# Building an attention row once and broadcasting it by DMA, instead of transposing a broadcast on TensorE

## The chip, the cores and the metric

The kernel runs on one core of a Trainium2 chip. The core has five engines that matter here: TensorE (PE, with its weight loads shown as PEld), VectorE (DVE), ScalarE (ACT), GpSimd (POOL) and SyncE (SP, which only issues DMA transfers here). The metric is the device time of one execution in microseconds; before the change it is 3412.09 us, the median of three runs (3411.46 to 3415.26). The profile is of another execution and spans 3416.2 us.

## The reference, cut to what matters

Four graph-attention layers run over `x` of shape (32, 512, 256): 32 batches of 512 tokens with 256 features, all float32. Each layer normalizes its input and adds its result to it. In shape, all four do this:

```python
h = maximum(layernorm(x), 0)
Wh = h @ W                               # 512 tokens x 256 features
s_i, s_j = Wh @ a1, Wh @ a2              # one number for each token
e = leaky_relu(s_i[:, None] + s_j[None, :])
e = where(mask, e, -inf)                 # mask: adjacency, the same for all batches
out = elu_or_relu(softmax(e, axis=-1) @ Wh)
x = x + out
```

Layer 2 does it with four heads of 64 features. Layer 3 has a small network around it and two attentions: one on 512 features without a mask, one on 256 with it.

The softmax weight before normalization, exp(leaky_relu(s_i + s_j)), is a maximum of two products of exponentials. A factor that depends on i alone cancels in the softmax, and a factor of j can be put on the rows of `Wh`. What is left for each pair is `max(R_i, T_j) * mask`: a row `R` over the tokens i, and a column `T` over the tokens j.

## The kernel before

Tokens lie on the 128 partitions in NT = 4 tiles, so `R` comes out of the value projection as a column: one number for each partition, in each of the four tiles. The weights `w[j, i]` need it along the free dimension and the same on all partitions. The kernel gets that from TensorE: it takes the column of one token tile, broadcasts it to 128 x 128 with a step of zero and transposes that against the identity. Four such transposes, one for each token tile, fill a PSUM bank with `R` (128 x 512). VectorE reads it there, four times, and writes the four tiles of `w`:

```python
def weights(r_col, t_col, masked=True):
    r = bank()                                             # one PSUM bank, of 8
    for t in range(NT):
        nc.tensor.transpose(r[:, t * P:(t + 1) * P], r_col(t).to_broadcast([P, P]), ident)
    wt = work.tile([P, NT, N], FP, tag="w", name="w", bufs=5)
    for j in range(NT):
        if masked:
            nc.vector.scalar_tensor_tensor(
                wt[:, j, :], r, t_col(j), maskT[:, j, :], op0=OP.max, op1=OP.mult)
        else:
            nc.vector.tensor_scalar(wt[:, j, :], r, t_col(j), None, op0=OP.max)
    return wt

def aggregate(p, wt, t, rhs):                              # the attention times the values
    for j in range(NT):
        nc.tensor.matmul(p, wt[:, j, t * P:(t + 1) * P], rhs(j), start=(j == 0), stop=(j == NT - 1))

def plain(hT, w):                                          # layers 0, 1 and the second of layer 3
    v = yield from values(hT, w)                           # projection; columns F.. hold the exponentials
    wt = weights(lambda t: v[:, t, F + 2:F + 3], lambda j: v[:, j, F + 1:F + 2])
    yield
    return v, wt
```

Layer 2 calls `weights` once for each of its four heads. The first attention of layer 3 calls it without a mask, and then goes on like this:

```python
    ys = []
    for t in range(NT):
        y, q = pair(), pair()
        # ... aggregate, reciprocal, two activations ...
        elu2_plus1(y, q)                                   # VectorE, ScalarE, and last GpSimd
        ys.append(y)
        yield
    for f in range(KH):                                    # 4 feature blocks
        p = bank()
        for t in range(NT):
            nc.tensor.transpose(p[:, t * P:(t + 1) * P],
                ys[t].rearrange("p a f -> p (a f)")[:, f * P:(f + 1) * P], ident)
        nc.vector.scalar_tensor_tensor(oT[:, f, :], p, -1.0, oT[:, f, :], op0=OP.add, op1=OP.add)
        # ...
```

Each batch is a Python generator that goes through the four layers and yields between steps. Four such streams run in turn, each started 20 rounds after the one before it, so that at the start one stream is alone, then two, then three:

```python
live = []
for i in range(NS):                                        # NS = 4
    live.append(stream(i))                                 # batches i, i + 4, i + 8, ...
    if i + 1 < NS:
        for _ in range(LEAD):                              # LEAD = 20
            for g in live:
                next(g)
# ... then all four in turn to the end
```

A scheduler then decides, when the kernel is built, in which order the instructions stand on each engine; each engine runs its own in that order. All DMA transfers are issued from SyncE: the inputs and weights at the start, then one load of `x` and one store of the output for each batch.

Of the kernel before, what the change touches and what calls it, by code (L numbers as in the profile page):

```python
# [19 lines left out]
FP = mybir.dt.float32  # L20
# [3 lines left out]
OP = mybir.AluOpType  # L24
# [3 lines left out]
P = 128  # L28
# [5 lines left out]
def fast(ctx, tc, flag, x, adj, w0, a0, w1, a1, w2, a2, mlp1_w, mlp1_b, mlp2_w, mlp2_b,  # L34
# [14 lines left out]
    psum = ctx.enter_context(tc.tile_pool(name="psum", bufs=1, space=bass.MemoryType.PSUM))  # L49

# [31 lines left out]
    def project(dst, block, kt, a_cols):  # L82

        ft, n = a_cols.shape[1], a_cols.shape[2]
        for k in range(kt):
# [3 lines left out]
            wT = work.tile([P, N], FP, tag="y", name="wT", bufs=8)  # L89
# [54 lines left out]
    raw2 = work.tile([P, KF, F], FP, tag="y2", name="raw2", bufs=4)  # L144
# [94 lines left out]
    def weights(r_col, t_col, masked=True):  # L239

        r = bank()
        for t in range(NT):
            nc.tensor.transpose(r[:, t * P:(t + 1) * P], r_col(t).to_broadcast([P, P]), ident)  # L243
        wt = work.tile([P, NT, N], FP, tag="w", name="w", bufs=5)
        for j in range(NT):
            if masked:
                nc.vector.scalar_tensor_tensor(  # L247
                    wt[:, j, :], r, t_col(j), maskT[:, j, :], op0=OP.max, op1=OP.mult
                )
            else:  # L250
                nc.vector.tensor_scalar(wt[:, j, :], r, t_col(j), None, op0=OP.max)
        return wt

    def pair():
        return work.tile([P, 2, F], FP, tag="y", name="y", bufs=8)
# [10 lines left out]
    def plain(hT, w):  # L266
        v = yield from values(hT, w)
        wt = weights(lambda t: v[:, t, F + 2:F + 3], lambda j: v[:, j, F + 1:F + 2])
# [20 lines left out]
    def layer0(xt):  # L289
        v, wt = yield from plain((yield from norm_t(xt)), W0)  # L290
        for t0 in range(0, NT, 2):
            r, q = pair(), pair()
# [18 lines left out]
    def layer2(xt):  # L311
# [15 lines left out]
        note(v.rearrange("p t h c -> p (t h) c")[:, :, D:])  # L327
        ys = [pair(), pair()]
        for h in range(NH):
            wt = weights(lambda t: v[:, t, h, D + 2:D + 3], lambda j: v[:, j, h, D + 1:D + 2])  # L330
# [12 lines left out]
        for i in range(2):  # L343
            y, q = ys[i], pair()
# [5 lines left out]
    def layer3(xt):  # L350
# [18 lines left out]
        wt = weights(lambda t: v[:, t, F + 2:F + 3], lambda j: v[:, j, F + 1:F + 2], masked=False)  # L369
        yield  # L370
        ys = []
        for t in range(NT):
            y, q = pair(), pair()
# [8 lines left out]
            ys.append(y)  # L382
            yield
        for f in range(KH):
            p = bank()
            for t in range(NT):
                nc.tensor.transpose(  # L387
                    p[:, t * P:(t + 1) * P], ys[t].rearrange("p a f -> p (a f)")[:, f * P:(f + 1) * P], ident
                )
            nc.vector.scalar_tensor_tensor(oT[:, f, :], p, -1.0, oT[:, f, :], op0=OP.add, op1=OP.add)  # L390
            if f % 2:
                yield
        rT = yield from linear_t(oT, WM2, b2, "rT")
        v, wt = yield from plain(rT, WHA)
        for t0 in range(0, NT, 2):
            y, q = pair(), pair()
# [489 lines left out]
```

## Time and profile before

| what | value |
|---|---|
| time, median of three | 3412.09 us |
| TensorE busy in the profile | 3314.6 us, 97% |
| VectorE, ScalarE, GpSimd busy | 50%, 40%, 17% |
| transposes that build R (line 243) | 1024 |
| VectorE operations that build w (lines 247 and 251) | 896 + 128 |
| DMA traffic | 40.67 MB, mean 12 GB/s |

In the lists that follow, a line such as `L243 PE MATMUL b<-ident,v` is a group of instructions: the source line, the engine, the operation, and output<-inputs by the program's names, `b` being a PSUM bank. After `x` comes the count, then the busy time in us and the mean duration of one in ns, then the idle time of that engine just before them and what ended it. The durations of neighbouring matmuls overlap, so a group's busy time can exceed what it takes in sequence. A float32 matmul is two instructions (two passes), and a transpose is one; so `L259`, the aggregation, counts 9216 for 4608 matmuls in the program. "PEld" is the load of the stationary operand, which overlaps the matmuls.

### The profile page before, as it was taken

The page shows a single profiled execution, that of the slowest core. Times are in us where ns is not written, and L with a number is a line of the kernel's source. Part 1 is how long each engine was busy: PE and PEld are TensorE (multiplying, and loading weights), DVE is VectorE, ACT ScalarE, POOL GpSimd, SP SyncE. Part 2 cuts the span into 40 slices and gives each one's busy share as a digit, 9 for nine tenths or more (in the row PEclk, how much of TensorE's full clock was granted, in tenths as well). Part 3 has the DMA queues.
Part 4 walks back from the last instruction along what each step waited for, and adds up shares of the span by engine and source line. Part 5 has one row for each costly group of instructions (what it writes and reads, how often), then busy time and mean ns, then how long its engine had stood idle before and what let it go on. Part 6 is the DMA issues. An engine that isn't in the chain of part 4 may idle for free.

```text
span 3416.2 us, 44221 instructions
## 1 busy us (share of the span) xinstructions
PE 3314.6 (97%) x17265; PEld 2750.0 (80%) x17265; DVE 1700.9 (50%) x4422; ACT 1380.6 (40%) x3281; POOL 571.7 (17%) x583
## 2 busy tenths in 40 slices
PE   6899999999999999999999999999999999999997
PEld 5688888788887887878878888788888788887875
DVE  3554563554644655446544455454653545635542
ACT  2234434444334434344334443444434444344433
POOL 0111111211112111121111121112201111112111
PEclk8899999999999999999999999999999999999999
DMA  2000000000000000000000000000000000000000
GB/s 80 1 1 13 13 1 13 13 13 13 1 13 13 13 13 1 13 19 7 13 13 1 25 7 7 13 1 25 13 1 13 11 16 13 1 13 7 7 7 14
DMA packets 41606, 40.67 MB, mean 12 GB/s; under 512 B 5296, under 2 KB 40624, under 8 KB 41392
## 3 DMA queue, kind: packets, MB, share of 16 engines
q1 hardware_dynamic: 41392, 37.77, 3.6%
q8 instruction: 140, 2.29, 0.3%
q14 instruction: 74, 0.61, 0.1%
HBM read 20.99 MB, written 16.78 MB: 11 GB/s over the span
## 4 chain that ended last, share of the span: by engine, by line
PE 87%; DVE 6%; ACT 3%; POOL 3%; issue 1%; DMA 0%; SPq 0%; POOLq 0%; ACTq 0%; DVEq 0%
PE b L259 43%; PE b L357 13%; PE b L234 11%; PE b L216 8%; PE b L317 3%; PE b L198 3%; PE b L243 3%; PE b L387 1%; DVE xn L190 1%; POOL y L287 1%; DVE st L182 1%; DVE x L281 1%; POOL rs L186 1%; PE b L405 1%; DVE y L280 1%
## 5 line engine op out<-in xcount | busy, mean ns | idle before, releaser
L259 PE MATMUL b<-v,w 128*128 128x257 f32 (+2 forms) x9216 | 1657.9, 337 | 19.2 <-DVE w L247 16.9
L259 PEld LDWEIGHTS b<-v,w 128*128 128x128 f32 x9216 | 1457.2, 194 | 218.5 <-issue 44.0
L247 DVE SCALAR_TENSOR_TENSOR w<-b,v,maskT 128x512 f32<-128x512 f32 x896 | 609.2, 744 | 37.3 <-PE b L243 37.3
L287 POOL TENSOR_TENSOR y<-y 128x512 f32<-128x512 f32 x192 | 243.4, 1268 | 1799.2 <-ACT y L286 1566.7
L263 DVE RECIPROCAL rden<-b 128x1 f32<-128x1 f32 (+1 forms) x640 | 101.9, 166 | 756.2 <-PE b L259 755.4
L357 PE MATMUL b<-WFC,oT 128*128 128x259 f32 (+1 forms) x2048 | 466.4, 380 | 0.0
L357 PEld LDWEIGHTS b<-WFC,oT 128*128 128x128 f32 x2048 | 381.9, 189 | 62.5 <-issue 8.1
L190 DVE TENSOR_SCALAR xn<-x,mv,rs 128x256 f32<-128x256 f32 x512 | 190.8, 432 | 153.1 <-POOL rs L186 153.1
L216 PE MATMUL b<-W,hT 128*128 128x259 f32 x1024 | 263.4, 402 | 2.1 <-ACT hT L199 2.0
L182 DVE BATCH_NORM_STATS2 st<-x 128x6 f32<-128x256 f32 x512 | 194.4, 406 | 98.3 <-POOL x L308 67.1
L234 PE MATMUL b<-hT,WM 128*128 128x512 f32 x512 | 240.8, 593 | 0.0
L234 PE MATMUL b<-oT,WM 128*128 128x512 f32 x512 | 232.2, 596 | 0.5 <-DVE oT L390 0.5
L216 PEld LDWEIGHTS b<-W,hT 128*128 128x128 f32 x1024 | 195.4, 200 | 34.2 <-ACT hT L199 7.3
L295 ACT ACTIVATE y<-b,rden 128x256 f32<-128x256 f32 x128 | 60.8, 475 | 395.6 <-DVE rden L263 395.6
L379 ACT ACTIVATE y<-b,rden 128x256 f32<-128x256 f32 x256 | 123.2, 481 | 222.7 <-DVE rden L263 173.1
L199 ACT ACTIVATE hT<-b 128x512 f32<-128x512 f32 x256 | 142.3, 595 | 143.7 <-PE b L198 142.5
L221 ACT ACTIVATE v<-b,v 128x256 f32<-128x256 f32 x384 | 182.5, 475 | 12.5
L234 PEld LDWEIGHTS b<-oT,WM 128*128 128x128 f32 x512 | 95.8, 191 | 95.4 <-issue 87.5
L285 DVE TENSOR_SCALAR y<-y 128x512 f32<-128x512 f32 x192 | 82.4, 429 | 178.5 <-ACT y L379 142.4
L364 ACT ACTIVATE v<-b,v 128x256 f32<-128x256 f32 x256 | 121.5, 475 | 117.8 <-PE b L357 113.6
L198 PE MATMUL b<-ident,xn 128*128 128x128 f32 x1024 | 145.0, 283 | 19.1 <-DVE xn L190 19.1
L286 ACT ACTIVATE y<-y,minus 128x512 f32<-128x512 f32 x192 | 138.8, 723 | 57.3 <-DVE y L285 41.4
(99 smaller groups left out, 2892.8 us busy)
## 6 DMA issues: line engine op xcount, KB each, us to landing
x<-in_x_dram SPq DMA_DIRECT2D x32, 512.0 KB, 3.8
out_dram<-x SPq DMA_DIRECT2D x32, 512.0 KB, 2.9
adj<-in_adj_dram SPq DMA_DIRECT2D x1, 1024.0 KB, 8.1
WM<-in_L_gnn_mlp_w_dram SPq DMA_DIRECT2D x2, 512.0 KB, 5.4
WFC<-in_L_gnn_W_fc_dram SPq DMA_DIRECT2D x2, 512.0 KB, 5.7
W<-in_L_gnn_W_dram SPq DMA_DIRECT2D x2, 256.0 KB, 7.8
raw<-in_L_gnn_W_dram SPq DMA_DIRECT2D x1, 256.0 KB, 5.6
WHA<-in_L_gnn_W_hand_dram SPq DMA_DIRECT2D x1, 256.0 KB, 6.2
```

Source lines behind the costliest of these rows:

```text
L182: nc.vector.bn_stats(st[:, t, :], xt[:, t, :])
L190: nc.vector.tensor_scalar(xn[:, t, :], xt[:, t, :], mv[:, t, 0:1], rs[:, t:t + 1], op0=OP.subtract, op1=OP.mult)
L198: nc.tensor.transpose(p[:, t * P:(t + 1) * P], xn[:, t, k * P:(k + 1) * P], ident)
L199: nc.scalar.activation(hT[:, k, :], p, AF.Relu)
L216: nc.tensor.matmul(ps[:, :F + 3], hT[:, k, t * P:(t + 1) * P], w[:, k, :], start=(k == 0), stop=(k == KF - 1))
L221: nc.scalar.activation(v[:, t, :F], ps[:, :F], AF.Copy, scale=pj)
L234: nc.tensor.matmul(p, w[:, k, f * P:(f + 1) * P], inT[:, k, :], start=(k == 0), stop=(k == kt - 1))
L247: nc.vector.scalar_tensor_tensor(wt[:, j, :], r, t_col(j), maskT[:, j, :], op0=OP.max, op1=OP.mult)
L259: nc.tensor.matmul(p, wt[:, j, t * P:(t + 1) * P], rhs(j), start=(j == 0), stop=(j == NT - 1))
L286: nc.scalar.activation(q, q, AF.Exp, bias=minus1)
L287: nc.gpsimd.tensor_tensor(r, r, q, op=OP.add)
L357: nc.tensor.matmul(ps[c][:, :n], oT[:, k, t * P:(t + 1) * P], WFC[:, k, c * (F + 3):c * (F + 3) + n], start=(k == 0), stop=(k == KH - 1),)
```

## The change

`R` is transposed once for all token tiles, and the spreading over the partitions is left to a DMA. A new helper `spread` takes the four columns of `R` (16 in layer 2: four tiles by four heads) as one 128 x n operand, transposes it into n rows of 128, has ScalarE copy them to SBUF, and stores them in a DRAM buffer. `weights` then reads that buffer back with a DMA whose source is broadcast over the 128 partitions, so that `r` lies in SBUF (256 KB over all partitions). It is meant to take the repeated transposes from TensorE and the bank for `R` from PSUM. There is a yield between `spread` and `weights`, so that other streams may run meanwhile.

To make room in SBUF, the tag `y` goes from 8 buffers to 6, `q` gets a tag of its own with 3, and a weight buffer used at the start moves to another tag. In layer 3 the transposes of `y` are done after each token tile, and no longer for all four at the end. The numbers of matmuls there are the same.

```diff
+    dram = ctx.enter_context(tc.tile_pool(name="dram", bufs=1, space=bass.MemoryType.DRAM))
...
-            wT = work.tile([P, N], FP, tag="y", name="wT", bufs=8)
+            wT = work.tile([P, N], FP, tag="y", name="wT", bufs=6)
...
-    raw2 = work.tile([P, KF, F], FP, tag="y2", name="raw2", bufs=4)
+    raw2 = work.tile([P, KF, F], FP, tag="hT", name="raw2", bufs=3)
...
-    def weights(r_col, t_col, masked=True):
-
-        r = bank()
-        for t in range(NT):
-            nc.tensor.transpose(r[:, t * P:(t + 1) * P], r_col(t).to_broadcast([P, P]), ident)
+    def spread(cols):
+
+        n = cols.shape[1]
+        p = bank()
+        nc.tensor.transpose(p[:n, :P], cols, ident)
+        s = work.tile([P, P], FP, tag="row", name="row", bufs=3)
+        nc.scalar.copy(s[:n, :], p[:n, :P])
+        rows = dram.tile([n, P], FP, tag=f"row{n}", name=f"row{n}", bufs=2 * NS)
+        nc.sync.dma_start(rows, s[:n, :])
+        return rows
+
+    def weights(row, t_col, masked=True):
+
+        r = work.tile([P, N], FP, tag="r", name="r", bufs=6)
+        nc.sync.dma_start(r.rearrange("q (t p) -> q t p", p=P), row.partition_broadcast(P))
...
-    def pair():
-        return work.tile([P, 2, F], FP, tag="y", name="y", bufs=8)
+    def pair(tag="y"):
+        return work.tile([P, 2, F], FP, tag=tag, name=tag, bufs=6 if tag == "y" else 3)
...
     def plain(hT, w):
         v = yield from values(hT, w)
-        wt = weights(lambda t: v[:, t, F + 2:F + 3], lambda j: v[:, j, F + 1:F + 2])
+        r = spread(v[:, :, F + 2])
+        yield
+        wt = weights(r, lambda j: v[:, j, F + 1:F + 2])
         yield
... (layer 2)
+        rows = spread(v[:, :, :, D + 2].rearrange("p t h -> p (t h)")).rearrange("(t h) p -> h t p", h=NH)
+        yield
         for h in range(NH):
-            wt = weights(lambda t: v[:, t, h, D + 2:D + 3], lambda j: v[:, j, h, D + 1:D + 2])
+            wt = weights(rows[h], lambda j: v[:, j, h, D + 1:D + 2])
... (layer 3, first attention)
-        wt = weights(lambda t: v[:, t, F + 2:F + 3], lambda j: v[:, j, F + 1:F + 2], masked=False)
-        yield
-        ys = []
-        for t in range(NT):
-            y, q = pair(), pair()
+        r = spread(v[:, :, F + 2])
+        yield
+        wt = weights(r, lambda j: v[:, j, F + 1:F + 2], masked=False)
+        yield
+        for t in range(NT):
+            y, q = pair(), pair("q")
...
-            ys.append(y)
-            yield
-        for f in range(KH):
+            yield
             p = bank()
-            for t in range(NT):
+            for f in range(KH):
                 nc.tensor.transpose(
-                    p[:, t * P:(t + 1) * P], ys[t].rearrange("p a f -> p (a f)")[:, f * P:(f + 1) * P], ident
+                    p[:, f * P:(f + 1) * P], y.rearrange("p a f -> p (a f)")[:, f * P:(f + 1) * P], ident
                 )
-            nc.vector.scalar_tensor_tensor(oT[:, f, :], p, -1.0, oT[:, f, :], op0=OP.add, op1=OP.add)
-            if f % 2:
-                yield
+            o = oT[:, :, t * P:(t + 1) * P]
+            nc.vector.scalar_tensor_tensor(
+                o, p.rearrange("p (f c) -> p f c", c=P), -1.0, o, op0=OP.add, op1=OP.add
+            )
+            yield
```

With the added yields a batch has 62 steps, where it had 55; `LEAD` stays 20.

More of the change, by code (lines that the diff above doesn't have):

```diff
@@ L291, in layer0 @@
         for t0 in range(0, NT, 2):
-            r, q = pair(), pair()
+            r, q = pair(), pair("q")
             for i in range(2):
@@ L343, in layer2 @@
         for i in range(2):
-            y, q = ys[i], pair()
+            y, q = ys[i], pair("q")
             nc.scalar.activation(q, y, AF.Exp)
@@ L395, in layer3 @@
         for t0 in range(0, NT, 2):
-            y, q = pair(), pair()
+            y, q = pair(), pair("q")
             for i in range(2):
```

## The prediction

> **What bounds the kernel now.** I read the busy shares first, then the chain of waits, then the groups by line, then a stretch of the timeline, and last the waits and the DMA landings.
>
> ```profile
> span 3416.2 us, 44221 instructions
> ...
> PE 3314.6 (97%) x17265; PEld 2750.0 (80%) x17265; DVE 1700.9 (50%) x4422; ACT 1380.6 (40%) x3281; POOL 571.7 (17%) x583
> ...
> PE 87%; DVE 6%; ACT 3%; POOL 3%; issue 1%; DMA 0%; SPq 0%; POOLq 0%; ACTq 0%; DVEq 0%
> ...
> L243 PE MATMUL b<-ident,v 128*128 128x128 f32 x1024 | 145.7, 273 | 0.0
> ```
>
> ```profile
> 0.00:100.00 100.00, 62.31 (x260) 50.47 (x260) 38.48 (x107) 23.39 (x55) 10.48 (x17) 0.78 0.25 69
> 100.00:3300.00 3200.00, 3155.78 (x16546) 2625.93 (x16546) 1625.56 (x4228) 1313.13 (x3130) 542.30 (x550) 0.98 0.03 10
> 3300.00:3416.00 116.00, 96.55 (x463) 73.57 (x461) 36.91 (x89) 44.07 (x96) 18.96 (x16) 0.95 0.03 10
> ```
>
> TensorE sets the end: 97% busy, 87% of the chain. The second fence cuts the span in three (the columns are the stretch, its length, then PE, PEld, DVE, ACT and POOL busy): PE is idle 38 us in the first 100 us, 44 us in the 3200 us of the middle, and 19 us at the end. So every TensorE microsecond taken out of the middle is worth about one, and every new TensorE wait costs one. The other engines have room.
>
> The group of L243 is what the change attacks: the 1024 transposes that build the row R. Its busy sum, 145.7 us, is too high a price, since neighbouring matmuls overlap. The timeline gives the pace:
>
> ```profile
> 1697.30 0.60 PE L243 MATMUL b<-ident,v 128*128 128x128 f32 x4
> 1697.73 7.15 PE L259 MATMUL b<-v,w 128*128 128x257 f32 x48
> ...
> 1709.06 0.60 PE L243 MATMUL b<-ident,v 128*128 128x128 f32 x4
> 1709.50 1.92 PE L216 MATMUL b<-W,hT 128*128 128x259 f32 x8
> ```
>
> (start, length, what.) Four transposes start at 1697.30 and the next matmul at 1697.73; again 1709.06 and 1709.50. That is 0.435 us for four, 0.109 us each.
>
> ```profile
> DVE w L247 <- PE b L243: 37.3, 27, 2.8
> ```
>
> ```profile
> SPq L64 <- DMA out_dram<-x: 73.3, 27, 4.2
> ```
>
> ```profile
> x<-in_x_dram SPq DMA_DIRECT2D x32, 512.0 KB, 3.8
> out_dram<-x SPq DMA_DIRECT2D x32, 512.0 KB, 2.9
> ```
>
> ```profile
> L247 DVE SCALAR_TENSOR_TENSOR w<-b,v,maskT x896: 723/744/754, 56.5 to 3396.6; 128x512 f32<-128x512 f32 x180
> ...
> L281 DVE SCALAR_TENSOR_TENSOR x<-y,x x128: 661/684/1751, 62.9 to 3327.1; 128x512 f32<-128x512 f32 x128
> ...
> L251 DVE TENSOR_SCALAR w<-b,v x128: 741/746/753, 182.0 to 3364.3; 128x512 f32<-128x512 f32 x128
> ...
> L285 DVE TENSOR_SCALAR y<-y x192: 408/427/1228, 189.7 to 3404.4; 128x512 f32<-128x512 f32 x192
> ```
>
> The waits (total us, times, longest): building w waited for R only 27 times, so today R is at hand almost at once. A store that a later load depends on already costs the SyncE queue 2.7 us a time (73.3 / 27). The last column of the DMA lines is the median from issue to landing. The triples of the last fence are shortest, median and longest in ns.
>
> [...]
>
> [...] L251, from PSUM, 746 ns; L285, from SBUF at the same size, 427.
>
> [...] L281 (two SBUF inputs) has 1751 ns as its longest, median 684; L247 (one input in PSUM) never passes 754. After the change L247's successor has both inputs in SBUF.
>
> **The change, part by part.**
>
> *Removed from TensorE.* Per batch there are eight builds of w (one each in layers 0 and 1, four heads in layer 2, two in layer 3), each with four transposes: 32 batches x 8 x 4 = 1024. In their place are five one-shot transposes per batch (layer 2's four heads share one): 160. Net 864 x 0.109 = 94 us off TensorE, 2.8%.
>
> *Added elsewhere.* 160 ScalarE copies of 128 columns, about 0.27 us each by L90's COPY of 256 columns (373 ns): 43 us on an engine that is 40% busy. 160 stores of 2 or 8 KB and 256 broadcast reads of 256 KB, 416 issues at 0.37 us (the duration of a DMA issue in the trace) on a SyncE queue that is nearly idle: 154 us of 3400. The unmasked w of layer 3 reads SBUF and should fall from 746 to about 430 ns, 128 x 0.32 = 41 us off VectorE, not on the path.
>
> *The new lag.* From the transposes to the first use of w there were about 1.1 us (PE latency 0.16, one VectorE op 0.74, signals). Now: PE 0.16; waiting for ScalarE and its copy 0.5; store 1.9 (the output store's 2.9[...]); broadcast read 2.6 (the 512 KB load's shortest is 2.9, by its tile's answer, and this has half the bytes), or 3.4 for layer 2[...]; VectorE 0.74 and its queue 0.2; signals 0.2. Estimates: 6.3 us for ordinary layers, 7.1 for layer 2, 6.0 for the unmasked one (its first VectorE op is shorter).
>
> *What TensorE has to do meanwhile.* Nobody waits if other streams fill the lag. In the built program's own order on TensorE I added up the work between each new transpose and the first aggregation with its w, at the trace's pace (0.434 us for a 257-column float32 matmul, two passes; 0.22 for 65 columns; 0.86 for 512; 0.109 a transpose). The middle repeats every four batches. Its four layer-2 gaps hold 4.6, 6.2, 7.1 and 10.5 us; the four unmasked ones 7.1, 7.2, 8.9 and 9.3; the twelve ordinary ones 6.9 to 14.4. Against the lags only 4.6 and 6.2 fall short, by 2.5 and 0.9 us; with the next three w, which come 0.74 us apart, the cycle loses about 5 us. At the start one stream runs alone, then two, and at the end again: the gaps there are 0 to 4 us and each spread is exposed. The same sum, end to end: first 400 us 37 us of waits, middle 32, last 400 us 36, together 104. The order of the kernel before, with its lag of 1.1, gives 14, 0 and 14, so 76 us are new.
>
> *Layer 3's tail.* The back transposes of y now follow each token tile instead of coming in one block at the end. TensorE waited 23.8 us for GpSimd's y there; I take half of it, 10 us, as saved. The number of matmuls is the same.
>
> *The PSUM bank* that R occupied through four VectorE ops (3 us, 256 times) is free. Steady PE idle is only 44 us, so I give this nothing.
>
> *GpSimd collisions.* L281's mean is 845 ns against a median of 684: 0.16 us a time. On the 896 masked ops I take 0.1 us, 90 us of VectorE time, of which little is on the path; with the VectorE queue standing still behind a late R: +10 us together.
>
> Sum: 3412 - 94 + 76 - 10 + 10 = 3394; I predict **3395 us**, 0.5% faster.
>
> **The rivals.**
>
> *The lag is hidden (about 3330).* If store and read take 1.5 us less together than I think, the same sum over the order gives 60 us of waits instead of 104, and the end and start shrink too. For it: the gaps of the middle are mostly 7 us and more. Against it: no group of transfers in the trace has a median landing under 2.5 us (the 0.2 KB loads of the layer-2 vector a), and two must run one after the other.
>
> *A new wait takes the place of the work (3440 and more).* With a lag 1 us longer the sum is 145 us, 2 us longer 191: about 45 us per microsecond. For it: SyncE serves its queue in order, and one queue now carries rows of four streams, so a read may stand behind another row's store, or behind an output store that waits for GpSimd; and R's late arrival also stops VectorE's queue. Then 3435 to 3480.
>
> *VectorE becomes the bound.* 1701 + 90 - 41 = 1750 us, 51%: no. [...]
>
> **Range and chances.** The gain of 94 us is sure to within 10. The new waits are the doubt: a lag between 1 us shorter (69 us) and 1.5 longer (about 167) puts the time between 3359 and 3457; with 20 us for collisions and the layer-3 tail below, 3340 to 3460 holds it 8 times in 10. Over 2% faster means under 3344, which needs the lag hidden and the tail smoothed: 0.19. Slower than 3480 needs a lag over 2 us longer than mine: 0.13. Within 2%: 0.68.
>
> **What would show it.** The L244 group should have 160 transposes at about 0.11 us apart, and PE busy should fall by about 90 us. Store landings near 2 us and reads of 2.6 to 3.4 confirm the lag. PE's idle time by releaser should name VectorE's w in front of the aggregation, mostly in layer 2 (65-column form) and in the first and last 400 us; the middle's idle should stay near 70 us or less. The unmasked w should take about 430 ns and the masked ones keep 744 as median with a tail over 1 us. The prediction is wrong if landings are above 4 us, if PE's idle appears in the middle for other reasons (xn, y, a full PSUM), or if TensorE's pace itself changes.

## The result, and the profile after

| kernel | median, us | ratio to before, 95% interval |
|---|---|---|
| before, four runs | 3413.68 | |
| changed, four runs | 3689.33 | 1.0798 (1.0774 to 1.0822) |

The change costs 276 us, 8%. The page of the changed kernel (span and counts, the engines, TensorE's busy share and its granted clock in 40 slices, the chain's shares):

```profile
span 3688.0 us, 43451 instructions
...
PE 3409.4 (92%) x16401; PEld 2794.7 (76%) x16401; DVE 1698.4 (46%) x4422; ACT 1407.1 (38%) x3441; POOL 599.7 (16%) x583
...
PE   5889999989999899999999899998999999998885
...
PEclk7789999999999899999999999998999999998887
...
PE 72%; DVE 10%; DMA 6%; POOL 5%; ACT 4%; issue 2%; SPq 0%; POOLq 0%; ACTq 0%; DVEq 0%
```

TensorE has 864 instructions fewer, as meant, and is nevertheless busy 95 us longer (3409.4 against 3314.6). Its idle time went from 101.6 to 278.6 us (the span less busy). Against the 94 us by which its work should have shrunk, the rest of the work took 189 us more. So the 272 us between the two spans are -94 of work, +177 of idle time and +189 of pace. The clock row shows the pace: it falls under full speed at both ends and now and then in the middle. The span and mean granted clock of the kernel before and of this one:

```profile
core 0: 3416.2 us, clock 0.977
core 0: 3688.0 us, clock 0.927
```

The span times what the clock lacks to 1 is the work at full pace that was lost: 3416.2 x 0.023 = 79 us before, 3688.0 x 0.073 = 269 us here, 190 more. That is the 189 of pace, so next to nothing is left for anything but the clock to slow TensorE. By stretch (stretch, its length, busy time and instructions of each engine, clock, DMA share, GB/s):

```profile
0.00:100.00 100.00, 59.43 (x223) 47.44 (x224) 31.36 (x79) 20.88 (x49) 6.67 (x12) 0.74 0.25 74
100.00:3300.00 3200.00, 3039.93 (x14924) 2501.32 (x14923) 1547.56 (x4052) 1269.33 (x3118) 538.92 (x523) 0.95 0.10 29
3300.00:3688.00 388.00, 310.05 (x1258) 245.90 (x1256) 119.46 (x292) 116.86 (x274) 54.12 (x48) 0.83 0.06 20
```

The middle is idle for 160 us where it was idle for 44, at a clock of 0.95 where it had 0.98. The waits (total us, times, longest):

```profile
DVE w L258 <- DMA r<-row: 218.5, 64, 10.0
...
PE b L401 <- POOL y L300: 131.3, 62, 4.8
...
PE b L270 <- DVE w L258: 76.7, 46, 6.5
```

and the wait for y in the kernel before:

```profile
PE b L387 <- POOL y L287: 23.8, 24, 2.5
```

VectorE waits 218 us for R, and TensorE 77 us for w: the lag of the new route. But the largest wait of TensorE is another one: 131 us for GpSimd's y in front of layer 3's transposes (L401), where it waited 23.8 us before. Of the 177 us of new idle time 108 are for y (131.3 - 23.8) and 63 for w (82.6, both kinds of w together, against 19.3). The aggregation by its forms, and w on VectorE (shortest, median, longest in ns):

```profile
L270 PE MATMUL b<-v,w 128*128 128x257 f32 x4096 | 1012.1, 401 | 45.9 <-DVE w L258 34.5 <-DVE w L262 5.9 <-DVE rden L274 5.5
...
L270 PE MATMUL b<-v,w 128*128 128x65 f32 x4096 | 595.9, 311 | 43.1 <-DVE w L258 42.1
```

The 65-column form in the kernel before:

```profile
L259 PE MATMUL b<-v,w 128*128 128x65 f32 x4096 | 502.3, 281 | 13.1 <-DVE w L247 13.1
```

```profile
L258 DVE SCALAR_TENSOR_TENSOR w<-r,v,maskT x896: 715/744/1762, 61.9 to 3665.6; 128x512 f32<-128x512 f32 x180
L262 DVE TENSOR_SCALAR w<-r,v x128: 465/481/488, 214.4 to 3604.2; 128x512 f32<-128x512 f32 x128
```

The 65-column form, layer 2's, does the same work in 596 us of busy time that took 502 before. A stretch of TensorE's timeline shows both effects at once (start, length, what, in brackets the idle time before and what ended it), and the windows below it the clock there:

```profile
1242.80 10.67 PE L270 MATMUL b<-v,w 128*128 128x65 f32 x64
1258.23 1.12 PE L401 MATMUL b<-ident,y 128*128 128x128 f32 x4 [4.76 <-POOL y L300]
1259.14 6.93 PE L270 MATMUL b<-v,w 128*128 128x65 f32 x32
1265.87 1.91 PE L199 MATMUL b<-ident,xn 128*128 128x128 f32 x8
1267.57 5.01 PE L270 MATMUL b<-v,w 128*128 128x257 f32 x16
...
1274.17 1.03 PE L199 MATMUL b<-ident,xn 128*128 128x128 f32 x8
```

```profile
1258.00:1270.00 12.00, 11.77 (x50) 11.31 (x51) 1.36 (x4) 1.19 (x2) 0.17 (x1) 0.50 0.01 1
1270.00:1290.00 20.00, 18.98 (x82) 13.38 (x82) 9.09 (x23) 11.64 (x31) 2.53 (x3) 0.99 0.04 13
```

TensorE stands 4.76 us for y. After that the same 32 passes of 65 columns that take 3.68 us elsewhere in the trace take 6.93, and eight transposes 1.91 instead of 1.03: half pace, at a granted clock of 0.50, for 12 us. Nothing is waited for in those 12 us, so they count as busy time. A wait of 3 us or more on TensorE occurs 3 times in the trace before and 39 times here (after the first 60 us), and each of the 39 is followed by half clock within 6 us. In all TensorE spends 539 us of this trace at half clock, 232 of them in the 65-column form; before it was 160 and 47.

The lag itself, in the chain of waits around one spread (start, length, what):

```profile
1196.74 0.25 ACT row L246
...
1197.00 4.35 DMA row<-row
...
1201.40 3.37 DMA r<-row
...
1204.79 0.76 DVE w L258
...
1205.69 0.66 PE b L270 x2
```

Its transpose had started at 1196.16, so R took 9.5 us to the first use. SyncE's own timeline shows what the store ran beside (start, duration of the issue, what):

```profile
1195.94 0.37 SPq L65 DMA_DIRECT2D x<-in_x_dram  x1
1197.00 0.32 SPq L248 DMA_DIRECT2D row<-row  x1
1201.40 0.36 SPq L254 DMA_DIRECT2D r<-row  x1
```

The store of R (layer 2's 16 rows, 8 KB) was issued 1.06 us behind a 512 KB load of x and took 4.35 us. Six of the 32 stores of this size stand 0.4 to 1.1 us behind such a load, and the next read on the queue came 2.9 to 4.4 us after them; for the other 26 it came after 2.2 us at most.

### The profile page after: what moved, and what is told of

Read it like the earlier page. It is cut to its first block, busy times and chain, and to the rows that moved or that the text cites. A ratio compares the mean times of both kernels' runs of the same rounds, so it can differ in the third digit from the quotient of the medians.

```text
span 3688.0 us, 43451 instructions
## 1 busy us (share of the span) xinstructions
PE 3409.4 (92%) x16401; PEld 2794.7 (76%) x16401; DVE 1698.4 (46%) x4422; ACT 1407.1 (38%) x3441; POOL 599.7 (16%) x583
## 4 chain that ended last, share of the span: by engine, by line
PE 72%; DVE 10%; DMA 6%; POOL 5%; ACT 4%; issue 2%; SPq 0%; POOLq 0%; ACTq 0%; DVEq 0%
PE b L270 36%; PE b L235 10%; PE b L372 10%; PE b L217 7%; DVE w L258 5%; DMA r<-row 4%; PE b L199 3%; POOL y L300 3%; PE b L330 2%; PE b L401 2%; DVE st L183 1%; DMA row<-row 1%; DVE xn L191 1%; POOL rs L187 1%; ACT q L299 1%
## 5 line engine op out<-in xcount | busy, mean ns | idle before, releaser
L270 PE MATMUL b<-v,w 128*128 128x257 f32 (+2 forms) x9216 | 1811.7, 359 | 89.0 <-DVE w L258 76.7
L270 PEld LDWEIGHTS b<-v,w 128*128 128x128 f32 x9216 | 1596.6, 213 | 312.7 <-issue 113.7
L258 DVE SCALAR_TENSOR_TENSOR w<-r,v,maskT 128x512 f32<-128x512 f32 x896 | 657.7, 776 | 218.7 <-DMA r<-row 218.5
L300 POOL TENSOR_TENSOR y<-y,q 128x512 f32<-128x512 f32 x192 | 258.8, 1348 | 1823.6 <-ACT q L299 1688.3
L395 ACT ACTIVATE q<-b,rden 128x256 f32<-128x256 f32 x256 | 121.0, 473 | 514.9 <-DVE rden L274 478.6
L401 PE MATMUL b<-ident,y 128*128 128x128 f32 x512 | 92.0, 309 | 131.4 <-POOL y L300 131.3
L401 PEld LDWEIGHTS b<-ident,y 128*128 128x128 f32 x512 | 65.3, 155 | 158.8 <-POOL y L300 151.3
L321 POOL TENSOR_TENSOR x<-x,y 128x512 f32<-128x512 f32 x64 | 85.1, 1330 | 611.0 <-ACT y L319 494.5
L222 ACT ACTIVATE v<-b,v 128x256 f32<-128x256 f32 x384 | 179.6, 475 | 10.6
L308 ACT ACTIVATE q<-b,rden 128x256 f32<-128x256 f32 x128 | 60.6, 473 | 318.1 <-DVE rden L274 316.7
L299 ACT ACTIVATE q<-q,minus 128x512 f32<-128x512 f32 x192 | 138.7, 722 | 78.6 <-DVE q L298 67.5
```

What stands on the lines that cost most here:

```text
L222: nc.scalar.activation(v[:, t, :F], ps[:, :F], AF.Copy, scale=pj)
L258: nc.vector.scalar_tensor_tensor(wt[:, j, :], r, t_col(j), maskT[:, j, :], op0=OP.max, op1=OP.mult)
L299: nc.scalar.activation(q, q, AF.Exp, bias=minus1)
L300: nc.gpsimd.tensor_tensor(r, r, q, op=OP.add)
L401: nc.tensor.transpose(p[:, f * P:(f + 1) * P], y.rearrange("p a f -> p (a f)")[:, f * P:(f + 1) * P], ident)
```

## The experiments

The theory: a wait of TensorE can cost twice, once as idle time and once as slow work after it; and the waits come from two parts of the change that have nothing to do with each other, R's lag (w) and layer 3's in-line transposes (y). The rivals: that the lag alone is the cause and the waits for y follow from it; that TensorE is slowed by something else (PSUM, SBUF, the DMA traffic); that the buffers moved about (y from 8 to 6, q with 3 of its own) are what stalls y. Each ratio below is against the kernel before, run on the same chip (3416 to 3418 us), with its 95% interval.

### One part of the change at a time

**In-line transposes alone**, in the kernel before:

```diff
-            ys.append(y)
             yield
-        for f in range(KH):
             p = bank()
-            for t in range(NT): ... transpose(..., ys[t] block f, ident)
-            nc.vector.scalar_tensor_tensor(oT[:, f, :], p, -1.0, ...)
+            for f in range(KH): ... transpose(..., y block f, ident)
+            nc.vector.scalar_tensor_tensor(oT[:, :, t * P:(t + 1) * P], p, -1.0, ...)
+            yield
```

> The kernel before with one part of the change alone: in layer 3 the transposes of y follow each token tile instead of one block after all four. R is still built by TensorE. If the in-line form is by itself what makes TensorE wait for GpSimd's y (131 us in the changed kernel, 24 before), the same wait should show here at 90 to 130 us, with a lower granted clock, and the time should be 3500 to 3600. If those waits are only a consequence of the late R (VectorE's queue standing still behind the DMA), this kernel should be within 20 us of 3412 and the wait for y under 40 us.

3438.05 us, 1.0064 (1.0047 to 1.0080). This lies between the two expectations. The in-line transposes do not save anything; they cost 20 us, with 62 us of waits for y:

```profile
PE b L384 <- POOL y L287: 62.4, 44, 3.3
```

TensorE's idle time grew by 33 us, but its busy time fell by 15: here the new waits did not cost twice.

**The changed kernel without the read.** The transpose, the copy and the store stay; w is computed from a constant row that is always there. The kernel leaves out the broadcast read and what depends on it:

```diff
-        r = work.tile([P, N], FP, tag="r", name="r", bufs=6)
-        nc.sync.dma_start(r.rearrange("q (t p) -> q t p", p=P), row.partition_broadcast(P))
+        r = r_const
```

> The changed kernel without the broadcast read: w is built from a constant row in SBUF that is written once, so the output is not the reference's; the one-shot transposes, copies and stores stay, and so does the in-line layer 3. It takes away the whole lag of R. If the lag and what it drags behind it is the cause of the loss, the time falls below the kernel before, to 3300 to 3350, and TensorE's waits for w and for y both go. If the in-line transposes are the cause of their part, the waits for y stay near 100 us and the time is 3450 to 3560.

3444.1 us, 1.0079 (1.0062 to 1.0095). The waits for w are gone, those for y remain, 110 us. So the waits for y do not follow from R's lag, and even with R at hand at no cost in time this kernel would not have been faster than the kernel before.

**Each with and without the other.** With an offset of 22 rounds (the block form was not run at 20) four kernels differ in two things: transposes of y in a block or in-line, and R by the read or constant. With the form go its steps (60 in the block form, 62 in-line) and its buffers.

```diff
-    LEAD = 20
+    LEAD = 22
```

> The changed kernel with one number changed: each stream starts 22 rounds after the one before it, and not 20. A batch has 62 steps after the change, so 3 x 20 = 60 puts the first and the fourth stream two steps apart, nearly in step; 66 puts them 4 apart the other way, as they were before the change (60 against 55, 5 apart). If two streams in step are what piles up the waits, the time should fall by 60 us or more from 3689 and the wait for y by half. If the in-line transposes or the lag are the cause, it should stay within 40 us of 3689.

> The changed kernel with layer 3's transposes of y put back into one block after the four token tiles (y has 8 buffers again and r has 4, to fit), and with 22 rounds between the streams, since at 20 the buffers of y do not suffice for two streams in step. Read against the run with 22 rounds alone. If the in-line form is the cause of TensorE's waits for y, these fall from about 130 us to under 40, the granted clock rises by 0.02 or more, and the time falls by 120 to 200 us against that run, to about 3480 to 3560. If the late R is the cause, the waits for y move to other places and the time changes by less than 60 us.

> The block form of layer 3 at 22 rounds, and no broadcast read (w from a constant row, so the output is not the reference's): both suspects taken away at once, with the one-shot transposes, copies and stores kept. Against the block form with the read it gives the cost of the lag without in-line transposes. If the work taken off TensorE is worth 94 us and only the lag and the in-line form eat it, the time is 3310 to 3360, with TensorE's clock back at 0.975 or above. If something else in the change costs time, it stays above 3400.

> The in-line form without the broadcast read, at 22 rounds (w from a constant row, output not the reference's): the missing corner of four kernels at 22 rounds, of which three are measured: in-line with the read 3738, block with the read 3484, block without the read 3314. If the in-line form and the late R each cost their own, this one is at 3738 - 3484 + 3314 = 3568. If the in-line transposes are harmless as long as VectorE is not held by the DMA, it is below 3400; the run at 20 rounds (3444) suggests something between.

| offset 22 | R constant (no read) | R by the read |
|---|---|---|
| block | 3313.67, 0.970 (0.9684 to 0.9716) | 3484.46, 1.0190 (1.0173 to 1.0207) |
| in-line | 3497.28, 1.0234 (1.0217 to 1.0251) | 3738.06, 1.0941 (1.0922 to 1.0959) |

Either part alone costs about as much as the other, 171 and 184 us, and the two together 424, 70 more than their sum; simple addition had put the in-line kernel without the read at 3568, and it took 3497. Without both the kernel takes 3314 us: the removal of the transposes is worth what it was meant to be. That kernel has the added yields too. The offset of 22 costs the changed kernel 49 us (3738 against 3689), so it is not slow because its first and fourth streams run nearly in step at 20. (In the block form y has 8 buffers and r 4; a run further down says what that does.)

### What the clock does

Three small kernels, with nothing of the attention in them. **The first** runs 16 stretches of 60 float32 matmuls of 512 columns (120 passes) with a wait between them that a chain of n ScalarE copies makes:

```python
for n in (1, 2, 3, 4, 5, 6, 8, 10, 1, 2, 3, 4, 5, 6, 8, 10):
    for m in range(60): nc.tensor.matmul(p, ident, c, start=True, stop=True)     # 128 x 512
    for m in range(n): nc.scalar.copy(...)                                       # the next c
```

> A measurement of TensorE's clock alone: sixteen stretches of 60 float32 matmuls (120 passes of 512 columns, about 52 us), and between them TensorE waits for a chain of 1, 2, 3, 4, 5, 6, 8 and 10 ScalarE copies, each list gone through twice; nothing else runs, and the attention is left out. If waits lower the granted clock, matmuls after a wait above some length run at twice their time for some microseconds and those after shorter waits do not; from the traces of the two kernels I expect the step near 3 us, that is from 4 or 5 copies on, and 3 to 7 us of lost time after each. If the clock was lower in the changed kernel for another reason, the first matmuls after every wait here are as fast as the later ones.

From its timeline, the same wait of 3.27 us twice and the shortest that lost anything:

```profile
165.67 53.46 PE L48 MATMUL b<-c,ident 128*128 128x512 f32 x120 [1.97 <-ACT c L51]
...
276.80 54.52 PE L48 MATMUL b<-c,ident 128*128 128x512 f32 x120 [3.27 <-ACT c L51]
...
727.73 51.77 PE L48 MATMUL b<-c,ident 128*128 128x512 f32 x120 [3.27 <-ACT c L51]
```

51.77 us (0.431 a pass) is the full pace, the shortest of the 16 stretches; the waits, up to 6.5 us long, cost 0 to 2.8 us of it. That is less than was expected, and too little: 36 more waits of 3 us at 2.8 us would be 101 us, not 189. **The second** has only short matmuls, 240 of 65 columns (480 passes) a stretch:

> The clock measurement again, with 65-column matmuls in place of 512 (240 matmuls, 480 passes, about 52 us a stretch), as layer 2's heads have them; the attention is left out. After waits of about 2 us and more the 512-column stretches lost 1.7 to 2.8 us when they lost anything. In the changed kernel 65-column work stayed at half clock for 12 us after one wait of 4.8 us. If short matmuls keep the clock down for longer after a wait, the stretches here lose 4 us and more; if not, they lose 2 to 3 us as before, and the long slow stretches of the kernel need another reason.

```profile
107.18 102.66 PE L48 MATMUL b<-c,ident 128*128 128x65 f32 x480 [0.95 <-ACT c L52]
```

Every stretch takes 102.66 us, whatever the wait before it: 0.214 us a pass, twice what a pass takes at its best (below). **The third** puts 60 long matmuls, then the wait, then 240 short ones:

> Clock measurement, attention left out: 60 matmuls of 512 columns to bring TensorE to full pace, then a wait of 0, 2, 4, 6 or 8 ScalarE copies (0 to about 5 us), then 240 matmuls of 65 columns, the list gone through twice. If 65-column work keeps a clock that is up and only cannot raise it again, the stretches without a wait or after a short one take about 53 us and those after a long wait about 103. If it loses the clock by itself, all take 95 to 103. If the wait costs only a few us whatever follows, all take 53 to 57 and the half pace of the pure 65-column run had another reason.

```profile
57.96 53.71 PE L55 MATMUL s<-c,ident 128*128 128x65 f32 x480
...
165.07 53.81 PE L55 MATMUL s<-c,ident 128*128 128x65 f32 x480 [1.32 <-ACT c L51]
...
273.63 100.97 PE L55 MATMUL s<-c,ident 128*128 128x65 f32 x480 [2.62 <-ACT c L51]
374.96 53.21 PE L48 MATMUL b<-c,ident 128*128 128x512 f32 x120 [0.36 <-ACT c L56]
...
593.50 102.66 PE L55 MATMUL s<-c,ident 128*128 128x65 f32 x480 [5.22 <-ACT c L51]
```

In these runs 480 short passes kept full pace where they began with it, and never got back to it where they began without. Straight after long matmuls, or after a wait of 1.3 us, they run at full pace for 480 passes (53.7 us, 0.112 each). After a wait of 2.6 us or more they run at half pace for all 100 us, and only the next long matmuls go back to full pace, losing 1.3 to 2.8 us over it (53.21 here against 51.77). The repeat in the same run gave the same lengths within 0.1 us. Ahead of long matmuls a wait of 1.97 us lost 1.7 us both times, and one of 3.27 us lost 2.8 us once and nothing the other time; ahead of short ones 2.62 us was enough for half pace both times, 47 us lost over 480 passes (100.97 against 53.71). In the changed kernel each of the 39 waits of 3 us or more is followed by half clock, mostly for 5 to 12 us, and layer 2 has 4096 passes of 65 columns.

### Why y is late

**More buffers**, in the changed kernel at offset 22:

```diff
-            wT = work.tile([P, N], FP, tag="y", name="wT", bufs=6)
+            wT = work.tile([P, N], FP, tag="y", name="wT", bufs=8)
-        r = work.tile(..., tag="r", name="r", bufs=6)
+        r = work.tile(..., tag="r", name="r", bufs=4)
-        return work.tile([P, 2, F], FP, tag=tag, name=tag, bufs=6 if tag == "y" else 3)
+        return work.tile([P, 2, F], FP, tag=tag, name=tag, bufs=8 if tag == "y" else 3)
```

> The changed kernel at 22 rounds with the buffers of the block form (8 of y and 4 of r, instead of 6 and 6), in-line transposes kept. If the in-line form is slow because y has too few buffers, this should come close to the block form's 3484. If the form itself makes TensorE wait, it stays within 40 us of 3738.

3733.05 us, 1.0920 (1.0902 to 1.0938), with 149 us of waits for y, where six buffers gave 3738 and 150. The number of y buffers is not the cause.

**The changed kernel with R on TensorE**: its in-line form, its added yields and its buffers, but no DMA for R. First at offset 22, then at 20:

```diff
-        r = spread(v[:, :, F + 2])
+        r = lambda t: v[:, t, F + 2:F + 3]
         yield
...
+        r = bank()
+        for t in range(NT):
+            nc.tensor.transpose(r[:, t * P:(t + 1) * P], row(t).to_broadcast([P, P]), ident)
```

> The changed kernel at 22 rounds with its yields, buffers and in-line layer 3, but R built on TensorE as before. If yields and offsets (which streams stand in layer 2 while another waits in layer 3) make the in-line form dear, it is near 3590 (3497, the same without R's DMA, plus 94 us of transposes). If the transposes that build R had been filling the gaps in front of y, it is near the 3438 of the in-line form alone.

> The run with the changed kernel's yields, buffers and in-line layer 3 and R on TensorE, at 20 rounds instead of 22. If the added yields make the in-line form dear at either offset, it is near 3538 (3444 without R's DMA at 20 rounds, plus 94 us of transposes). If the offset of 22 alone does it, it is near the 3438 of the in-line form with the old yields.

3585.44 us, 1.0497 (1.0479 to 1.0514), and 3557.24, 1.0399 (1.0366 to 1.0433). With not one transfer for R the kernel is already 140 us slower. The in-line form in the old steps cost 20, so the yields or q's three buffers make up the rest. **The yields without the buffers**, q again from the shared tag of 8:

```diff
-        return work.tile([P, 2, F], FP, tag=tag, name=tag, bufs=6 if tag == "y" else 3)
+        return work.tile([P, 2, F], FP, tag="y", name="y", bufs=8)
```

> The kernel before with the transposes of y after each token tile and with the added yields alone (62 steps a batch, offset 20); R on TensorE, q out of the shared tag of 8 buffers as before. With 57 steps the in-line form took 3438 us; with 62 steps and q in three buffers of its own it took 3557. If the added yields make the waits for y long: 3557 within 15 us, waits for y near 116 us. If q's three buffers do (each y waits for a q to come free): 3438 within 15, waits for y near 62. In between: both have a part.

3542.42 us, 1.0370 (1.0353 to 1.0388):

```profile
PE b L390 <- POOL y L290: 116.9, 56, 4.3
```

With the in-line form it is the yields. (The 15 us left to 3557 are not resolved: that kernel's own runs lie between 3546 and 3569.) The yields compute nothing; they move the four streams against each other. With 62 steps a batch and streams 20 steps apart, other parts of the layers fall together than with 57. With the block form they cost nothing that shows: without the read, at offset 22, it has the same five yields and takes 3314 us, about what the kernel before would take without its 864 transposes (3416 - 94 = 3322). It is the two together; and since the yields came with R's new route, the two parts of the change are less separate than the theory has them.

The built order on TensorE shows what follows. I added up the work that stands between a token tile's last aggregation and the transposes of its y, at the pace used in the prediction: with 57 steps its median is 6.1 us, and 4 of 128 such gaps have under 1 us; with 62 steps the median is 4.0 us, and 26 of 128 have under 1 us (3.6 us and 26 in the changed kernel; aggregations and transposes are paired in their order). With next to nothing between, TensorE waits for the reciprocal, two activations and the ELU on three engines, up to 4.8 us.

### Using the DMA only where the lag is covered

All of these have R's new route in part. **An offset of 15** for the block form, and **a hybrid** that takes R by TensorE, and without the added yields, in the first and last four batches, when few streams run:

```diff
-    LEAD = 22
+    LEAD = 15
```

> The block form with 15 rounds between the streams: a batch has 60 steps, so the four streams are spread evenly, and the start and the end are shorter (45 rounds instead of 66). If the ramps are the larger part of what is left, it gains 40 to 80 us on the 3484 of 22 rounds; if the waits are spread over the middle and depend on how the streams are offset, the middle's waits change and the time can go either way.

```diff
-            yield from layer(xt)
+            yield from layer(xt, NS <= b < B - NS)      # True: R by the DMA, False: four transposes
```

> The block form at 22 rounds, but the first four and the last four of the 32 batches build R on TensorE as before, and only the 24 in the middle by DMA. It takes the lag out of the start and the end, where one, two or three streams run and nothing fills it, and gives back 8 x 27 transposes (24 us). If the ramps cost what the traces of the changed kernel say (more than 60 us of waits with half of the clock behind them), the time falls from 3484 to 3390 to 3430. If the lag costs the same in the middle, it falls by less than 30 us.

3498.6 us, 1.0239 (1.0222 to 1.0256), and 3431.79, 1.0055 (1.0035 to 1.0075). The earlier start of the streams does not help. With the ends on TensorE again the block form is 53 us better than its 3484 (waits for w 58 us instead of 96), but as a whole it still gains nothing on the kernel before. **A second yield behind each spread**, to let more work in:

```diff
             r = spread(v[:, :, F + 2])
             yield
+            yield
```

> An attempt at a better version: R by DMA for the 24 batches in the middle, by TensorE for the first and last four, block form, and a second yield between spread and weights, so that three more steps of other streams come before w in the scheduler's order; 24 rounds between streams, since a batch has 65 steps then. If the middle's waits for w go, the time is 3350 to 3400, faster than both kernels. If the scheduler's order does not move the aggregation away from the spread, it stays at 3420 to 3450.

3440.37 us, 1.0068 (1.0051 to 1.0085). The waits for w fell to 27 us, as wanted, and those for y rose to 54 and for xn to 33: moving the streams again made others late.

**No new step at all: only heads 1 to 3 of layer 2.** In the kernel before, one spread ahead of head 0; head 0 still gets its R by transposes and covers the lag of the others with its own work. Layers 0, 1 and 3 are untouched:

```diff
+        rows = spread(v[:, :, :, D + 2].rearrange("p t h -> p (t h)")).rearrange("(t h) p -> h t p", h=NH)
         for h in range(NH):
-            wt = weights(lambda t: v[:, t, h, D + 2:D + 3], ...)
+            wt = weights(rows[h] if h in (1, 2, 3) else (lambda t: v[:, t, h, D + 2:D + 3]), ...)
```

> The kernel before, with R by DMA only for heads 1 to 3 of layer 2: one transpose and one store for all, head 0 and every other layer on TensorE as before, layer 3 and the number of yields as before. While head 0 is worked on, the lag of the other heads should be covered. Saved are 12 - 1 = 11 transposes for each batch, 32 x 11 x 0.109 = 38 us; if the lag is covered, the time is 3370 to 3390, faster than both kernels. If the reads of three heads, or VectorE held behind them, still make TensorE wait, it is 3410 or more.

3326.04 us, 0.9738 (0.9722 to 0.9754): 92 us faster than the kernel before, 363 faster than the changed one, and better than the 3370 to 3390 expected. TensorE's busy share and clock on the page, the 65-column form, and the transfers (count, size, median us from issue to landing):

```profile
PE 3226.8 (97%) x16913; PEld 2674.3 (80%) x16913; DVE 1713.0 (52%) x4422; ACT 1385.5 (42%) x3313; POOL 602.0 (18%) x583
...
PEclk7999999999999999999999999999999999999999
```

```profile
L276 PE MATMUL b<-v,w 128*128 128x65 f32 x4096 | 474.3, 273 | 0.9 <-DVE w L264 0.8
```

```profile
r<-row SPq DMA_DIRECT2D x96, 256.0 KB, 3.8
...
row<-row SPq DMA_DIRECT2D x32, 8.0 KB, 2.0
```

Store and read take 2.0 and 3.8 us, but TensorE waits only 0.9 us in front of the 65-column form. 352 transposes less are 38 us at 0.109; TensorE's busy time fell by 88. The other 50 us are pace: the mean clock went from 0.977 to 0.990, and the 65-column form from 502 to 474 us. Its idle time is nearly the same, 96 us against 102, and both have three waits of 3 us or more after the first 60 us. What went is a place that came back every 413 us, seven times, in the kernel before, with no long wait in it:

```profile
473.67 0.44 PE L259 MATMUL b<-v,w 128*128 128x65 f32 x2 [0.64 <-DVE w L247]
474.66 0.44 PE L259 MATMUL b<-v,w 128*128 128x65 f32 x2 [0.56 <-DVE w L247]
475.32 0.44 PE L259 MATMUL b<-v,w 128*128 128x65 f32 x2 [0.22 <-DVE w L247]
476.10 0.44 PE L387 MATMUL b<-ident,y 128*128 128x128 f32 x2 [0.34 <-POOL y L287]
...
476.74 5.66 PE L259 MATMUL b<-v,w 128*128 128x65 f32 x26
```

```profile
476.70:486.90 10.20, 10.20 (x42) 9.33 (x41) 1.73 (x5) 1.84 (x4) 0.00 (x0) 0.50 0.00 0
```

Four short waits, 1.76 us in all, stand among a few short passes, and 10.2 us at half clock follow: 7 x 10.2 / 2 = 36 of the 50 us. With heads 1 to 3 by DMA none of these seven is left. That the short waits brought them was not tried by itself.

**Head 0 as well**, the one whose lag nothing covers:

```diff
-            wt = weights(rows[h] if h in (1, 2, 3) else ...
+            wt = weights(rows[h] if h in (0, 1, 2, 3) else ...
```

> As the run with three heads, but head 0 by DMA too, so that its lag of about 7 us stands between the spread and the first aggregation of each layer 2. It saves 4 x 32 x 0.109 = 14 us more of transposes. If the exposed lag and the clock behind it are what the changed kernel pays for, it is 30 to 100 us slower than the run with three heads; if the scheduler covers it with other streams, it is 10 us faster.

3493.53 us, 1.0209 (1.0176 to 1.0242):

```profile
PE b L276 <- DVE w L264: 81.9, 57, 6.6
```

```profile
L276 PE MATMUL b<-v,w 128*128 128x65 f32 x4096 | 536.5, 289 | 78.1 <-DVE w L264 78.0
```

This is the cleanest measure of an exposed lag. One more head of each batch goes to the DMA, TensorE has 128 transposes less (14 us), and the kernel loses 167 us, more than the 30 to 100 expected: TensorE's idle time grew by 86 us, nearly all of it waits for w, and its busy time by 88 us, with less to do. The mean clock is 0.962; by the sum used above the two kernels lose 133 and 33 us to it, 100 us apart, and 88 + 14 = 102 are to be explained.

## Why the prediction was wrong, point by point

The runs at offset 20 give a ladder from the kernel before to the changed one, with TensorE's idle and busy time in the profile of each:

| kernel | time, us | step | PE idle, us | PE busy, us |
|---|---|---|---|---|
| before | 3417 | | 102 | 3315 |
| + in-line transposes of y | 3438 | +21 | 135 | 3300 |
| + the added yields | 3542 | +104 | 182 | 3360 |
| + the changed buffers of y and q | 3557 | +15 | 181 | 3387 |
| + spread for the transposes, R at hand | 3444 | -113 | 164 | 3280 |
| + R by the read (the changed kernel) | 3689 | +245 | 279 | 3409 |

The steps depend on their order, as the extra 70 us at offset 22 show, and so can their weights: the yields cost 104 us behind in-line transposes and nothing visible with the block. The step of 15 lies within the spread of that kernel's runs, and its idle and busy time are of a run of 3569 us.

- **"Net 864 x 0.109 = 94 us off TensorE"** was right: the step measures -113, and the 19 us beyond the transposes lie near the spread of the runs (3546 to 3569).
- **The new lag** was of the right size. In the run of heads 1 to 3 the stores landed after 2.0 us (1.9 assumed) and layer 2's reads after 3.8 (3.4 assumed); with head 0 as well the stores landed after 1.4. The changed kernel's profile gives no landing times, and the 4.35 above belongs to one of six late stores. Where VectorE waited for a read there, w started 3.33 us after the read's issue in layer 2 (median of 25 waits), 3.16 in the ordinary layers (39) and 3.46 for the unmasked w (21): the 2.6 assumed for the last two and the 1.9 for a store were the author's estimates, as was the 0.8 us more for layer 2, where 0.2 came against the ordinary layers. "104 together" of waits for w were predicted, and 83 us came (76.7 + 5.9): 24 in the first 400 us (37 predicted), 31 in the middle (32), 27 at the end (36). "Mostly in layer 2 (65-column form)" was half right: of the 89 us of idle time ahead of the aggregation 43 are in that form, 46 in the 257-column one.
- **The failed step: "every new TensorE wait costs one."** A microsecond of waiting cost about two where the new route's lag was exposed. The last step of the ladder shows it: 115 us more idle time and 129 us more busy time for the same work, 245 together, where the sum had 76. Head 0 says the same by itself: 86 idle and 88 busy. It is no fixed price: in-line transposes alone added 33 us of idle time and no slow work. The reason is the clock, whose mean accounts for the whole of the slow work (190 us by the clock, 189 by the busy times) and which the small kernels show apart from everything else. The prediction had named it only as the last thing that would make it wrong ("if TensorE's pace itself changes") and given it no term, although the profile before carried it in its clock row and in a mean of 0.977.
- **The second failed step: "Layer 3's tail ... I take half of it, 10 us, as saved."** The sign was wrong: the waits for y went from 23.8 us to 131.3. In-line transposes and yields together cost 125 us of time. The prediction summed the work between each transposed R and its first use in the built order, and never did so for y, where the same sum would have shown 26 of 128 gaps with under 1 us in them.
- **Collisions with GpSimd** were assumed at 0.1 us per masked w; the mean of 776 ns over a median of 744 makes 0.03. The tail to 1.76 us is there, and all 34 of the 896 operations that took over 0.8 us overlap one of GpSimd. In the trace before, 211 of the 896 of L247 overlap one and none took over 754 ns, while all 21 of L281's 128 that took 1.64 us or more do. The other way round, the 59 operations of GpSimd for y (L300) that overlap a masked w took 1.61 us at the median, 1.81 at most; the other 133 took 1.26 to 1.27. The unmasked w took 481 ns instead of "about 430" (1.55 times as fast as the 746 from PSUM), and is nowhere on the path.
- **The rivals.** "The lag is hidden" is what happens without the read and with the block: 3314 us, near its 3330, and with heads 1 to 3 it can be had for real. "A new wait takes the place of the work (3440 and more)" named the right kind of end, but for a lag 1 to 2 us longer; the lag was not longer. VectorE was no bound: 46%.

What stays open: why the two parts together cost 70 us more than each alone was not tried by itself (a clock already low that meets a second wait is an argument, not a finding). Nor was the block form run at 20 rounds, or the added yields alone in the kernel before.

## What to carry to other kernels

Price a wait on TensorE by its length and by what follows. Here 86 us of new idle time behind head 0's lag came with 88 us of slow work, and in the small kernels a wait of 2.62 us ahead of 480 short passes lost 47 us, while waits of 0.68 to 6.52 us ahead of 120 long passes lost 2.8 us at most. (Four short waits close together, 1.76 us in all, stood ahead of 10.2 us at half clock; that they brought it was not shown.) With the route by DMA for heads 1 to 3, whose lag work that was already there covered, the kernel was 92 us faster than the one before; with head 0 as well it was 76 us slower. So use such a route only behind work that is there and leave head 0 on the other, and add yields only with that in view: the five yields of each batch moved the other gaps too, the median work ahead of y's transposes from 6.1 us to 4.0. Before building, sum the work between producer and consumer in the built order for each edge that the change moves, not just for the one it is about.

## What the runs showed of the hardware

- In the kernel that has nothing else, float32 passes of 65 columns ran at half pace throughout: 0.214 us a pass for 102.66 us, 16 times over. After 512-column matmuls, with no wait or one of 1.32 us between, they kept full pace, 0.112 us a pass. In the trace that has short passes alone the clock reads 1.000 although the pace is half; where long ones precede them it reads 0.51 in the slow stretch.
- The loss after a wait did not follow from its length alone: in front of 512-column matmuls 1.97 us lost 1.7 us both times, 2.62 us nothing both times, 3.27 us 2.8 and then nothing.
- In the changed kernel the next read on the queue came later after an 8 KB store to DRAM that stood close behind a load: 2.9 to 4.4 us after the six stores issued 0.4 to 1.1 us behind a 512 KB load of x, and 2.2 us at most after the other 26. That the load is what holds them up was not tried by itself.
